# A four-layer graph network on one core: the last layer's weighted sums as seven products for eight, and its sums of weights as means

## The chip, the core and the metric

The kernel runs on one core of a Trainium2 chip. TensorE (PE) multiplies matrices out of SBUF into PSUM, VectorE (DVE) and ScalarE (ACT) work element by element on both memories, GpSimd (POOL) and SyncE (SP) here mostly issue DMAs. The metric is the device time of one execution, in microseconds (us); the time of a kernel is the median of several runs.

## What is computed

Four attention layers over a graph of 4096 nodes with 256 features each; after each one x becomes layernorm(x + layer(x)). The change concerns the fourth layer:

```python
def _L3_gnn_ref(features, adj, Wq, Wk):
    Qn = _cos_normalize(features @ Wq.T)          # 4096 x 128
    Kn = _cos_normalize(features @ Wk.T)
    raw_att = Kn @ Qn.T
    att = jnp.where(adj > 0, raw_att, NEG) * TEMP
    att = jax.nn.softmax(att, axis=1)
    prop_fea = att @ features                     # 4096x4096 @ 4096x256
    adj_mask = (jnp.sum(adj, axis=1) > 0).astype(features.dtype)[:, None]
    prop_fea = adj_mask * prop_fea + (1.0 - adj_mask) * features
    return (1.0 - KEEP_RATIO) * prop_fea + KEEP_RATIO * features   # KEEP_RATIO 0.5
x = _layernorm(x + _L3_gnn_ref(x, adj, Wq, Wk), axis=-1)
```

Every node is its own neighbour, so adj_mask is 1 and the last line before the layernorm is 1.5 x + 0.5 att @ x. The layernorm takes away each row's mean, so a constant added to all features of a row changes nothing in the output.

## The kernel before

All is in f32. The features stay in SBUF as X, 32 tiles of 128 nodes by 256 features, with a 257th column that holds 2.0. The nodes that are computed are taken in NB = 8 blocks of QW = 512 (QB = 4 tiles of 128); in each block a loop runs over all NT = 32 tiles of neighbours. A step of that loop, a unit (b, j), belongs to block b and tile j of neighbours.

In the fourth layer (`cosine_attention`, L887) a unit has two parts. `weights(b, j)` (L907) multiplies the turned keys and queries in T into a PSUM bank p of 128 neighbours by 512 nodes (L912), takes exp on ACT into a tile prob in SBUF (L916), and multiplies by the mask on DVE (L917). The mask is bf16; POOL loads it by DMA, four tiles at a time (`load_mask`, L849), into four buffers. `sums(b, j)` (L922) adds prob times features: for each of the block's four tiles k one matmul holds 128 by 128 of prob and streams X[:, j, :] of 257 columns (`one_sum`, L919). The 257th column gives twice the sum of the weights, which carries the factor 0.5. There are four accumulators acc0 to acc3 of one PSUM bank each. Two banks (pz) and two more (ps) serve the scores in turn; in block 0 only pz does.

The main loop (L982) calls weights for unit i and sums for unit i - LAG, with LAG = 2. After a block's last unit `outputs(b)` (L940) takes each accumulator: reciprocal of the sum (L931), multiply and add to 1.5 x (L932), mean and variance (L934, L935); then normalise (L176) and one store. 1.5 x was written to y by ACT (L994) eight units earlier. In the last block the sums of the last LAST = 4 units are held back and ordered by k, so that the first tiles are finished beside the last sums (`ending`, L947).

No order is written out for PE in this layer; a planner orders each engine's work, taking what is ready, and among that what comes first in the program. For `ending` DVE and ACT keep the program's order. Each engine works in order through what the planner gave it. The tiles of a pool are handed out in turn, and a tile is free for its next use when all reads of its last one are done.

The layer's start overlaps the end of the third (`additive_one`, L401): its outputs for the last block (`tail`), and `Cosine.prepare` for the last two blocks (L856). This turns X by DVE and DMA, multiplies by the weights w3_sb of the layer (L869), takes the rows' norms, and turns the result by DVE and DMA into T. w3_sb, 256 features by 128 query and 128 key columns, is loaded by `Cosine.start` (L836) in block 0 of the third layer. Each block of the third layer ends in `layernorm_block` (L182), which makes X's rows of mean 0 and variance 1.

Of the kernel before, what the change touches and what calls it, by code (L numbers as in the profile page):

```python
# [9 lines left out]
FP = mybir.dt.float32  # L10
# [3 lines left out]
AF = mybir.ActivationFunctionType  # L14
# [14 lines left out]
def kernel(  # L29
# [32 lines left out]
    def pool(stack, name, bufs, **kw):  # L62
        return stack.enter_context(tc.tile_pool(name=name, bufs=bufs, reuse_waits="tile", **kw))
# [118 lines left out]
    def layernorm_block(b, mv):  # L182
        normalise([X[:, b * QB + k, :D] for k in range(QB)], mv)

# [216 lines left out]
    def additive_one(w_sb, slope, tail, op, follow):  # L401
# [3 lines left out]
        with ExitStack() as lay:  # L405
# [68 lines left out]
            def outputs(b, k):  # L474
                if k == 0:
                    mvs[b] = fin.tile([P, QB, 2], FP, name="mv")
                add_elu(taken[b, k], b, k, mvs[b])
                if k == QB - 1:
                    layernorm_block(b, mvs[b])

            def even_bank():
                n = next(even) % QB
# [4 lines left out]
            with tc.manual_schedule(engines={mybir.EngineType.PE}):  # L487
                xTs = {0: turn(0), 1: turn(1)}
                project(0, xTs[0])
                project(1, xTs[1], [0, 1])  # L490
                fill_row(0)
                project(1, xTs[1], [2, 3])
                for i in range(len(units) + 1):
                    if i < len(units):
                        b, j = units[i]
                        weights(b, j)

                        if b == 0 and j // QB + 2 < NB:
# [329 lines left out]
    class Cosine:  # L828
# [7 lines left out]
        def start(self):  # L836
# [9 lines left out]
            load_w(self.w_sb[:, :, :P], wq3T, nc.sync)  # L846
            load_w(self.w_sb[:, :, P:], wk3T, nc.sync)

        def load_mask(self, b, m, seen=None):  # L849

            mask = self.mask[b, m] = self.masks.tile([P, self.MJ, QW], BF, name="mask")
            part = adjT.rearrange("(t p) i -> p t i", p=P)[:, m * self.MJ:(m + 1) * self.MJ, b * QW:(b + 1) * QW]
            with behind(seen) if seen is not None else nullcontext():
                nc.gpsimd.dma_start(mask, part)  # L854
# [30 lines left out]
                             nc.gpsimd if b < NB - 2 else nc.sync)  # L885

    def cosine_attention(co, tail):  # L887
        MJ = co.MJ

        LAST = 4  # L890
        T = [t.rearrange("p k (n i) -> p n k i", n=2) for t in co.T]
        with ExitStack() as lay:
            sb = pool(lay, "co_sb", LAST + 2)
            yp = pool(lay, "co_y", 2)
            co.turning = (pool(lay, "co_turn", 2), pool(lay, "co_squares", 1),
                          pool(lay, "co_turn_far", 2, space=bass.MemoryType.DRAM))

# [4 lines left out]
            acc, prob, y = {}, {}, {}  # L902

            def bank():
                return ps.tile([P, QW], FP, name="g")

            def weights(b, j):  # L907
                m = b, j // MJ
                if m not in co.mask:
                    co.load_mask(*m)  # L910
                p = bank() if b and j % 2 else pz.tile([P, QW], FP, name="p")
                nc.tensor.matmul(p.rearrange("p (k i) -> p k i", k=QB), T[j // QB][:, 0, j % QB], T[b][:, 1],  # L912
                                 start=True, stop=True)

                z = prob[b, j] = sb.tile([P, QW], FP, name="prob")
                nc.scalar.activation(z, p, AF.Exp)  # L916
                nc.vector.tensor_tensor(z, z, co.mask[m][:, j % MJ, :], OP.mult)  # L917

            def one_sum(b, j, k):  # L919
                nc.tensor.matmul(acc[b][k], prob[b, j][:, k * P:(k + 1) * P], X[:, j, :], start=(j == 0), stop=(j == NT - 1))  # L920

            def sums(b, j):  # L922
                if j == 0:
                    acc[b] = [pa.tile([P, D + 1], FP, name=f"acc{k}") for k in range(QB)]
                for k in range(QB):
                    one_sum(b, j, k)

            def sums_and_rest(b, k, mv):

                rden = fin.tile([P, 1], FP, name="rden1")  # L930
                nc.vector.reciprocal(rden, acc[b][k][:, D:])  # L931
                nc.vector.scalar_tensor_tensor(y[b][:, k, :], acc[b][k][:, :D], rden, y[b][:, k, :], OP.mult, OP.add)  # L932
# [14 lines left out]
            def ending(b):  # L947


                mv = {k: fin.tile([P, n, 2], FP, name=f"mv_end{k}") for k, n in ((0, 2), (2, 1), (3, 1))}  # L950
                roots = {}

# [10 lines left out]
                for k in range(QB):  # L963
                    for j in range(NT - LAST, NT):
                        one_sum(b, j, k)
                sums_and_rest(b, 0, mv[0][:, 0, :])
                sums_and_rest(b, 1, mv[0][:, 1, :])
                roots[0] = begin_root(mv[0])
                sums_and_rest(b, 2, mv[2][:, 0, :])
                finished(0, 2)  # L970
                roots[2] = begin_root(mv[2])
                sums_and_rest(b, 3, mv[3][:, 0, :])
                v, r, _ = begin_root(mv[3])
                finished(2, 1)
                end_root(v, r, 1)
                scale_row(y[b][:, 3, :], mv[3], r, 0)
                store(b, 3, 1, nc.scalar)

            units = [(b, j) for b in range(NB) for j in range(NT)]
            LAG = 2  # L980
            steps = {(0, j + n): (NB - 2 + b, step) for b, j in enumerate((1, 12)) for step, n in enumerate((0, 5, 8))}
            for i in range(len(units) + LAG):  # L982
                if i < len(units):
                    b, j = units[i]
                    weights(b, j)
                    if (b, j) == (0, 1):
                        tail(bank)
                    if (b, j) in steps:
                        co.prepare(bank, *steps[b, j])
                if i >= LAG:  # L990
                    b, j = units[i - LAG]
                    if j == NT - 8:
# [102 lines left out]
```

## Time and profile before

| | us |
|---|---|
| median of 3 runs | 2892.93 (2892.83 to 2893.68) |
| span of the profiled execution | 2890.8 |
| fourth layer, first score to the end of the span | from 2212.9 |
| score, one pass of 512 columns, 512 of them (L912) | 0.592 each |
| sum, one pass of 257 columns, 2048 of them (L920) | 0.380 each |
| exp of 512 (L916) | 0.597 each |
| mask multiplication of 512 (L917) | 0.690 each |
| last sum's start, last scaling's start, last store's issue | 2883.4, 2887.35, 2887.80 |

[...] one starts before the last has ended; so the work of PE is counted from starts to starts. A row of the profile names line, engine, operation, tiles written and read, shape and count; then the busy time in us and the mean of one in ns; after the second bar the idle time of that engine just before such instructions, and what ended it. PEld is the loading of the operand that PE holds. The granted clock is 0.999 of full speed over the span.

### The profile page before, as it was taken

What the parts mean: (1) busy time and instruction counts of PE and PEld (TensorE: products, weight loads), DVE (VectorE), ACT (ScalarE), POOL (GpSimd) and SP (SyncE); (2) the same over time, 40 slices, a digit from 0 to 9 for tenths busy, and PEclk for the clock granted to TensorE, in tenths of its full rate; (3) what the DMA queues carried; (4) which work ended last, traced back from release to release, by engine and by line L of the source; (5) the groups of instructions that cost most, each with busy time, mean ns of one, the idle gap of its engine ahead of it and who ended that gap; (6) DMA issues with size and microseconds to landing.
All of it is one profiled execution on the core that took longest, in us unless ns stands there. A gap on an engine that the chain in (4) does not pass through costs nothing.

```text
span 2890.8 us, 50566 instructions
## 1 busy us (share of the span) xinstructions
PE 2879.6 (100%) x20093; PEld 1548.7 (54%) x20093; DVE 1959.5 (68%) x2557; ACT 1652.8 (57%) x2582; POOL 945.9 (33%) x705
## 2 busy tenths in 40 slices
PE   9999999999999999999999999999999999999999
PEld 4333333333543333333333358888888777777776
DVE  8899999998777777777777765655667323333333
ACT  7899999997356666666666653444444222222222
POOL 0010010100068988989899870000002000000000
PEclk9999999999999999999999999999999999999999
DMA  7566667675269989889899885565566434333441
GB/s 206 103 139 137 142 134 145 138 133 92 88 138 192 183 187 196 181 187 190 182 193 188 181 178 133 164 184 158 159 185 178 76 57 58 59 58 59 59 59 30
DMA packets 237087, 398.04 MB, mean 138 GB/s; under 512 B 20929, under 2 KB 121265, under 8 KB 235954
## 3 DMA queue, kind: packets, MB, share of 16 engines
q0 software_dynamic: 104320, 184.06, 40.1%
q1 hardware_dynamic: 132112, 210.36, 23.7%
q8 instruction: 157, 2.57, 0.3%
q14 instruction: 80, 0.66, 0.1%
q10 hardware_dynamic: 418, 0.40, 0.0%
HBM read 328.60 MB, written 32.58 MB: 125 GB/s over the span
## 4 chain that ended last, share of the span: by engine, by line
PE 99%; DVE 1%; ACT 0%; DMA 0%; issue 0%; SPq 0%; DVEq 0%
PE acc L293 23%; PE acc L920 15%; PE acc L697 15%; PE p L664 15%; PE acc L464 8%; PE g L464 8%; PE p L912 4%; PE g L912 3%; PE g L579 2%; PE g L196 1%; PE pv L598 1%; PE acc L869 1%; PE acc L196 1%; PE g L118 1%; PE g L305 0%; PE p L734 0%
## 5 line engine op out<-in xcount | busy, mean ns | idle before, releaser
L676 DVE TENSOR_TENSOR prob<-p,mask 128x1024 f32<-128x1024 f32 x512 | 624.0, 1223 | 209.4 <-ACT p L666 203.6
L666 ACT ACTIVATE p<-p,shift 128x1024 f32<-128x1024 f32 x512 | 556.2, 1088 | 325.2 <-PE p L664 324.4
L293 PE MATMUL acc<-prob,V 128*32 128x512 f32 x6144 | 664.0, 593 | 1.1 <-DVE prob L283 1.1
L683 POOL TENSOR_TENSOR den<-den,prob 128x1024 f32<-128x1024 f32 x248 | 626.4, 2526 | 73.9 <-DVE prob L676 66.6
L280 ACT ACTIVATE prob<-row,dst 128x512 f32<-128x512 f32 x1020 | 633.1, 712 | 0.1
L283 DVE SCALAR_TENSOR_TENSOR prob<-prob,mask 128x2048 f32<-128x2048 f32 x256 | 582.7, 2287 | 24.2 <-ACT prob L280 21.3
L664 PE MATMUL p<-qT,kT 64*64 64x512 f32 x4096 | 532.7, 590 | 0.8 <-DVE prob L676 0.8
L697 PE MATMUL acc<-prob,V 64*64 64x512 f32 x4096 | 531.8, 590 | 0.0
L920 PE MATMUL acc<-X,prob 128*128 128x257 f32 x2048 | 485.4, 380 | 0.0
L920 PEld LDWEIGHTS acc<-X,prob 128*128 128x128 f32 x2048 | 389.2, 190 | 161.6 <-issue 112.3
L917 DVE TENSOR_TENSOR prob<-prob,mask 128x512 f32<-128x512 f32 x256 | 176.7, 690 | 405.6 <-ACT prob L916 405.4
L293 PEld LDWEIGHTS acc<-prob,V 128*32 128x32 f32 x6144 | 197.8, 110 | 452.6 <-issue 431.9
L91 POOL COPY tick<-prob 128x1 f32<-128x1 f32 x35 | 40.2, 1150 | 996.0 <-DVE prob L283 644.5
L456 ACT ACTIVATE e<-row,dst 128x512 f32<-128x512 f32 x256 | 184.1, 721 | 241.7 <-DVE prob L458 212.7
L697 PEld LDWEIGHTS acc<-prob,V 64*64 64x64 f32 x4096 | 156.0, 133 | 285.2 <-issue 277.9
L664 PEld LDWEIGHTS p<-qT,kT 64*64 64x64 f32 x4096 | 154.6, 133 | 277.2 <-issue 261.4
L458 DVE SCALAR_TENSOR_TENSOR prob<-e,mask 128x512 f32<-128x512 f32 x256 | 175.5, 686 | 169.8 <-PE acc L464 92.4
L854 POOL DMA_DIRECT2D mask<-in_adjT x64 | 48.1, 751 | 585.2 <-DVE prob L917 523.6
L689 POOL DMA_DIRECT2D den<-prob x240 | 233.2, 972 | 15.7 <-DVE prob L676 6.7
L916 ACT ACTIVATE prob<-p 128x512 f32<-128x512 f32 x144 | 85.7, 596 | 258.4 <-PE p L912 244.3
L464 PE MATMUL acc<-V,prob 128*128 128x257 f32 x1024 | 225.1, 380 | 0.0
L464 PE MATMUL g<-V,prob 128*128 128x257 f32 x1024 | 223.7, 380 | 0.0
(165 smaller groups left out, 1937.1 us busy)
## 6 DMA issues: line engine op xcount, KB each, us to landing
mask<-in_adjT SPq DMA_DIRECT2D x256, 512.0 KB
den<-prob POOLq DMA_DIRECT2D x240, 512.0 KB, 5.1
mask<-edges SPq DMA_DIRECT2D x512, 64.0 KB
mask<-in_adjT POOLq DMA_DIRECT2D x64, 512.0 KB, 5.7
edges<-in_adj POOLq DMA_DIRECT2D x32, 512.0 KB, 9.8
far<-squares SPq DMA_DIRECT2D x16, 512.0 KB
den<-prob SPq DMA_DIRECT2D x16, 512.0 KB
row<-far SPq DMA_DIRECT2D x7, 1024.0 KB
```

Of the source, the lines that this page charges most:

```text
L280: nc.scalar.activation(z[:, h, :], r, AF.Relu, bias=-1.0, scale=dst[:, j, h:h + 1])
L283: nc.vector.scalar_tensor_tensor(z, z, 1.0, mask[m][:, j % MJ, :].unsqueeze(1).to_broadcast([P, H, QW]), OP.add, OP.mult)
L293: nc.tensor.matmul(acc[b][h * G:(h + 1) * G, n, :], part, prob[b, j][:, h, :], start=(j == 0), stop=(j == NT - 1))
L464: nc.tensor.matmul(acc[b][k][:, :D + 1], prob[b, j][:, k * P:(k + 1) * P], V[:, j, :], start=(j == 0), stop=(j == NT - 1))
L664: nc.tensor.matmul(p[c * d:(c + 1) * d, r, :], kT[half, c, at:at + d], qT[half, c, cols], start=True, stop=True)
L666: nc.scalar.activation(p, p, AF.Exp, bias=shift)
L676: nc.vector.tensor_tensor(z, p, mask[m][:, j % MJ, :].unsqueeze(1).to_broadcast([P, KC, QW]), OP.mult)
L683: nc.gpsimd.tensor_tensor(to, to, flat, OP.add)
L689: nc.gpsimd.dma_start(to, flat, accum_op=OP.add)
L697: nc.tensor.matmul(acc[b][c][r * d:(r + 1) * d, :], V[half, j, r * d:(r + 1) * d], prob[b, j][half, r, :], start=(j == 0), stop=(j == NH - 1))
L912: nc.tensor.matmul(p.rearrange("p (k i) -> p k i", k=QB), T[j // QB][:, 0, j % QB], T[b][:, 1], start=True, stop=True)
L920: nc.tensor.matmul(acc[b][k], prob[b, j][:, k * P:(k + 1) * P], X[:, j, :], start=(j == 0), stop=(j == NT - 1))
```

## The change

The third layer leaves X with rows of mean 1 instead of 0 (`lift`: the subtracted mean is lowered by the variance plus epsilon, times the inverse root). From the weights w3_sb `centre` subtracts the mean over the features, so that queries and keys are what they were. Since features now have mean 1, the mean over a row of weights times features is the sum of the weights; the column of 2.0 isn't multiplied any more in this layer.

The sums are formed the other way round: features are held and weights streamed, so an accumulator has 128 features by 512 nodes, turned against before. For a pair g of neighbour tiles (even and odd), the two tiles, two halves of the features and two halves of the block's nodes make a product of 2 by 2 blocks; seven products of combinations of the halves replace the eight. `mix_features` forms four combinations of the features once, in block 0, and keeps them; `weights(b, g)` forms four of the weights for each pair on DVE. The accumulator is one tile of four banks, of which seven halves are used. `parts` adds these up into the four quarters of the result, `turned` turns them back by eight transposes into two ps banks, `halves_of_inverse` takes the mean of each row for the reciprocal. LAG is 4 units, LAST 3 pairs.

```diff
-    def normalise(ys, mv):
+    def normalise(ys, mv, lift=False):
         v, r, n = begin_root(mv)
         end_root(v, r, n)
+        if lift:
+
+            nc.vector.tensor_tensor(v, v, r, OP.mult)
+            nc.vector.tensor_tensor(mv[:, :, 0], mv[:, :, 0], v, OP.subtract)
...
+                        if (b, j) == (0, 12):
+                            follow.centre(bank())
...
+        def centre(self, pm):
+
+            w = self.w_sb
+            for c in range(KC):
+                nc.tensor.matmul(pm[:, :2 * P], ones, w[:, c, :], start=(c == 0), stop=(c == KC - 1))
+            for c in range(KC):
+                nc.vector.scalar_tensor_tensor(w[:, c, :], pm[:, :2 * P], -1.0 / D, w[:, c, :], OP.mult, OP.add)
...
+            sb = pool(lay, "co_sb", LAST + 1)
...
+            def mix_features(q):
+
+                x = X[:, 4 * q:4 * q + 4, :D].rearrange("p (g n) (h f) -> p g n h f", n=2, h=2)
+                t = mixed[q] = keep.tile([P, 2, 4, P], FP, name=f"mixed{q}")
+                nc.vector.tensor_tensor(t[:, :, 0, :], x[:, :, 0, 1, :], x[:, :, 0, 0, :], OP.subtract)
+                nc.vector.tensor_tensor(t[:, :, 1, :], x[:, :, 1, 1, :], t[:, :, 0, :], OP.add)
...
+            def scores(b, j):
...
                 p = bank() if b and j % 2 else pz.tile([P, QW], FP, name="p")
...
+                if j % 2 == 0:
+                    prob[b, j // 2] = sb.tile([P, 2, QW], FP, name="prob")
+                nc.scalar.activation(prob[b, j // 2][:, j % 2, :], p, AF.Exp)
+
+            def weights(b, g):
+
+                if b == 0 and g % 2 == 0:
+                    mix_features(g // 2)
+                z, lo = prob[b, g], 2 * g % MJ
+                nc.vector.tensor_tensor(z, z, co.mask[b, 2 * g // MJ][:, lo:lo + 2, :], OP.mult)
+                s = mix[b, g] = sb.tile([P, 4, HW], FP, name="mix")
+                nc.vector.tensor_tensor(s[:, :2, :], z[:, 0, :].rearrange("p (h i) -> p h i", h=2), z[:, :, HW:],
+                                        OP.subtract)
+                nc.vector.tensor_tensor(s[:, 2, :], z[:, 0, :HW], s[:, 1, :], OP.subtract)
+                nc.vector.tensor_tensor(s[:, 3, :], z[:, 1, :HW], s[:, 2, :], OP.subtract)
+
+            def product(b, g, n):
...
+                at, half, w, a = ((3, 0, even[:, :P], z[:, 0, :HW]), (0, 0, odd[:, :P], z[:, 1, :HW]),
+                                  (0, 1, t[:, 1], s[:, 2]), (1, 0, t[:, 0], s[:, 1]), (1, 1, odd[:, P:], s[:, 3]),
+                                  (2, 0, t[:, 2], s[:, 0]), (2, 1, t[:, 3], z[:, 1, HW:]))[n]
+                nc.tensor.matmul(acc[b][:, at, half * HW:(half + 1) * HW], w, a, start=(g == 0 and half == 0),
+                                 stop=(g == NP - 1), skip_group_check=True)
+
+            def first_parts(b):
+                a = acc[b]
+                one = cp.tile([P, HW], FP, name="one")
+                nc.scalar.copy(one, a[:, 3, :HW])
+                r = cp.tile([P, 2, HW], FP, name="r")
+                nc.vector.tensor_tensor(r, one.unsqueeze(1).to_broadcast([P, 2, HW]),
+                                        a[:, 0, :].rearrange("p (h i) -> p h i", h=2), OP.add)
+                return r, cp.tile([P, 2, HW], FP, name="u")
+
+            def parts(b):
+
+                a = acc[b]
+                r, u = first_parts(b)
+                nc.vector.tensor_tensor(u, r[:, 1:, :].to_broadcast([P, 2, HW]), a[:, 1:3, :HW], OP.add)
+                nc.vector.tensor_tensor(r[:, 1, :], u[:, 1, :], a[:, 1, :HW], OP.add)
+                nc.vector.tensor_tensor(u, u, a[:, 1:3, HW:], OP.add)
+                return r, u
+
+            def turned(r, u, h):
+
+                po = bank().rearrange("p (k f) -> p k f", f=D)
+                for k in range(2):
+                    for c, quarter in enumerate((r[:, 0], u[:, 0]) if h == 0 else (u[:, 1], r[:, 1])):
+                        nc.tensor.transpose(po[:, k, c * P:(c + 1) * P], quarter[:, k * P:(k + 1) * P], ident)
+                return po
...
             def outputs(b):
+                r, u = parts(b)
                 mv = fin.tile([P, QB, 2], FP, name="mv")
-                for k in range(QB):
-                    sums_and_rest(b, k, mv[:, k, :])
+                for h in range(2):
+                    po = turned(r, u, h)
+                    rden = halves_of_inverse(po)
+                    for k in (2 * h, 2 * h + 1):
+                        rest(b, k, po, rden, mv[:, k, :])
                 normalise([y[b][:, k, :] for k in range(QB)], mv)
                 store(b, 0, QB, nc.sync)
...
-                for k in range(QB):
-                    for j in range(NT - LAST, NT):
-                        one_sum(b, j, k)
...
+                for n in range(5):
+                    for g in range(NP - LAST, NP):
+                        product(b, g, n)
+                r, u = first_parts(b)
+                nc.vector.tensor_tensor(u[:, 0, :], r[:, 1, :], a[:, 1, :HW], OP.add)
+                nc.vector.tensor_tensor(u[:, 0, :], u[:, 0, :], a[:, 1, HW:], OP.add)
+                po = turned(r, u, 0)
+                for n in (5, 6):
+                    for g in range(NP - LAST, NP):
+                        product(b, g, n)
+                rden = halves_of_inverse(po)
+                for k in range(2):
+                    rest(b, k, po, rden, mv[0][:, k, :])
                 roots[0] = begin_root(mv[0])
...
-            LAG = 2
+            LAG = 4
...
-                    if i - LAG < len(units) - LAST:
-                        sums(b, j)
+                    if i - LAG < len(units) - 2 * LAST:
+                        for n in range(7)[:4] if j % 2 == 0 else range(7)[4:]:
+                            product(b, j // 2, n)
                         if j == NT - 1:
                             outputs(b)
```

`halves_of_inverse` is a reduction over the 256 features of two tiles at once, a multiplication and a reciprocal; `rest` is the multiply and add, the mean and the variance of one tile, as in `sums_and_rest` before. In `ending` the second half follows in the same way: three additions of 256 elements, four transposes, reduction, two times `rest`.

More of the change, by code (lines that the diff above doesn't have):

```diff
@@ L174, in scale_row, with layernorm_block @@
         nc.vector.tensor_scalar(y, y, mv[:, k, 0:1], r[:, k:k + 1], OP.subtract, OP.mult)
-    def normalise(ys, mv):
+    def normalise(ys, mv, lift=False):
         v, r, n = begin_root(mv)
         end_root(v, r, n)
+        if lift:
+            nc.vector.tensor_tensor(v, v, r, OP.mult)
+            nc.vector.tensor_tensor(mv[:, :, 0], mv[:, :, 0], v, OP.subtract)
         for k, y in enumerate(ys):
             scale_row(y, mv, r, k)
-    def layernorm_block(b, mv):
-        normalise([X[:, b * QB + k, :D] for k in range(QB)], mv)
+    def layernorm_block(b, mv, lift=False):
+        normalise([X[:, b * QB + k, :D] for k in range(QB)], mv, lift)
     def additive_values(xT, b, groups, w_sb, V, src, dst, H, slope):
@@ L478, in outputs @@
                 if k == QB - 1:
-                    layernorm_block(b, mvs[b])
+                    layernorm_block(b, mvs[b], lift=True)
             def even_bank():
@@ L888, in cosine_attention @@
         MJ = co.MJ
-        LAST = 4
+        NP = NT // 2
+        HW = QW // 2
+        LAST = 3
         T = [t.rearrange("p k (n i) -> p n k i", n=2) for t in co.T]
         with ExitStack() as lay:
-            sb = pool(lay, "co_sb", LAST + 2)
+            keep = pool(lay, "co_mixed", 1)
+            sb = pool(lay, "co_sb", LAST + 1)
             yp = pool(lay, "co_y", 2)
+            cp = pool(lay, "co_parts", 1)
             co.turning = (pool(lay, "co_turn", 2), pool(lay, "co_squares", 1),
@@ L901, in cosine_attention @@
             ov = out.rearrange("(t p) d -> p t d", p=P)
-            acc, prob, y = {}, {}, {}
+            mixed, acc, prob, mix, y = {}, {}, {}, {}, {}
             def bank():
                 return ps.tile([P, QW], FP, name="g")
[L907 to L910, printed above, removed]
+            def mix_features(q):
[3 more added lines that the diff above has]
+                nc.vector.tensor_tensor(t[:, :, 1, :], x[:, :, 1, 1, :], t[:, :, 0, :], OP.add)
+                nc.vector.scalar_tensor_tensor(t[:, :, 2, :], x[:, :, 1, 1, :], -1.0, x[:, :, 0, 1, :],
+                                               OP.mult, OP.subtract)
+                nc.vector.tensor_tensor(t[:, :, 3, :], x[:, :, 1, 0, :], t[:, :, 1, :], OP.subtract)
+            def scores(b, j):
+                if (b, j // MJ) not in co.mask:
+                    co.load_mask(b, j // MJ)
                 p = bank() if b and j % 2 else pz.tile([P, QW], FP, name="p")
@@ L913, in weights @@
                                  start=True, stop=True)
[L915 to L924, printed above, removed]
-                for k in range(QB):
-                    one_sum(b, j, k)
@@ L928, in sums_and_rest @@
[L928 to L932, printed above, removed]
+                if j % 2 == 0:
[11 more added lines that the diff above has]
+                nc.vector.tensor_tensor(s[:, 3, :], z[:, 1, :HW], s[:, 2, :], OP.subtract)
@@ new lines, in product @@
+            def product(b, g, n):
+                z, s, t = prob[b, g], mix[b, g], mixed[g // 2][:, g % 2]
+                even, odd = X[:, 2 * g, :D], X[:, 2 * g + 1, :D]
+                at, half, w, a = ((3, 0, even[:, :P], z[:, 0, :HW]), (0, 0, odd[:, :P], z[:, 1, :HW]),
[3 more added lines that the diff above has]
+                                 stop=(g == NP - 1), skip_group_check=True)
@@ new lines, in turned, with halves_of_inverse @@
+            def turned(r, u, h):
[4 more added lines that the diff above has]
+                return po
+            def halves_of_inverse(po):
+                rden = fin.tile([P, 2], FP, name="rden2")
+                nc.vector.tensor_reduce(rden, po, AX.X, OP.add)
+                nc.vector.tensor_scalar_mul(rden, rden, 2.0 / D)
+                nc.vector.reciprocal(rden, rden)
+                return rden
@@ L933, in sums_and_rest, with rest @@
+            def rest(b, k, po, rden, mv):
+                nc.vector.scalar_tensor_tensor(y[b][:, k, :], po[:, k % 2, :], rden[:, k % 2:k % 2 + 1], y[b][:, k, :],
+                                               OP.mult, OP.add)
                 st = fin.tile([P, 6], FP, name="bn")
@@ L947, in ending @@
             def ending(b):
+                a = acc[b]
                 mv = {k: fin.tile([P, n, 2], FP, name=f"mv_end{k}") for k, n in ((0, 2), (2, 1), (3, 1))}
@@ L961, in finished @@
                     store(b, k, n, nc.sync)
-                for k in range(QB):
-                    for j in range(NT - LAST, NT):
-                        one_sum(b, j, k)
-                sums_and_rest(b, 0, mv[0][:, 0, :])
-                sums_and_rest(b, 1, mv[0][:, 1, :])
+                for n in range(5):
[11 more added lines that the diff above has]
+                    rest(b, k, po, rden, mv[0][:, k, :])
                 roots[0] = begin_root(mv[0])
-                sums_and_rest(b, 2, mv[2][:, 0, :])
+                nc.vector.tensor_tensor(u[:, 1, :], r[:, 1, :], a[:, 2, :HW], OP.add)
+                nc.vector.tensor_tensor(r[:, 1, :], u[:, 1, :], a[:, 1, :HW], OP.add)
+                nc.vector.tensor_tensor(u[:, 1, :], u[:, 1, :], a[:, 2, HW:], OP.add)
+                po = turned(r, u, 1)
                 finished(0, 2)
+                rden = halves_of_inverse(po)
+                rest(b, 2, po, rden, mv[2][:, 0, :])
                 roots[2] = begin_root(mv[2])
-                sums_and_rest(b, 3, mv[3][:, 0, :])
-                v, r, _ = begin_root(mv[3])
+                rest(b, 3, po, rden, mv[3][:, 0, :])
+                v, w, _ = begin_root(mv[3])
                 finished(2, 1)
-                end_root(v, r, 1)
-                scale_row(y[b][:, 3, :], mv[3], r, 0)
+                end_root(v, w, 1)
+                scale_row(y[b][:, 3, :], mv[3], w, 0)
                 store(b, 3, 1, nc.scalar)
             units = [(b, j) for b in range(NB) for j in range(NT)]
-            LAG = 2
+            LAG = 4
             steps = {(0, j + n): (NB - 2 + b, step) for b, j in enumerate((1, 12)) for step, n in enumerate((0, 5, 8))}
@@ L984, in cosine_attention @@
                     b, j = units[i]
-                    weights(b, j)
+                    scores(b, j)
+                    if j % 2:
+                        weights(b, j // 2)
                     if (b, j) == (0, 1):
@@ L991, in cosine_attention @@
                     b, j = units[i - LAG]
+                    if j == 0:
+                        acc[b] = pa.tile([P, 4, QW], FP, name="acc")
                     if j == NT - 8:
```

## The prediction

> **What bounds the kernel now.** I read the page's busy shares and its chain first, then the fourth layer by windows, then the chain in order of time, then the timeline of one block's end. From the page, the busy shares, the chain by engine, and the two costly groups of this layer:
>
> ```profile
> PE 2879.6 (100%) x20093; PEld 1548.7 (54%) x20093; DVE 1959.5 (68%) x2557; ACT 1652.8 (57%) x2582; POOL 945.9 (33%) x705
> ...
> PE 99%; DVE 1%; ACT 0%; DMA 0%; issue 0%; SPq 0%; DVEq 0%
> ...
> L920 PE MATMUL acc<-X,prob 128*128 128x257 f32 x2048 | 485.4, 380 | 0.0
> ...
> L917 DVE TENSOR_TENSOR prob<-prob,mask 128x512 f32<-128x512 f32 x256 | 176.7, 690 | 405.6 <-ACT prob L916 405.4
> ```
>
> TensorE (PE) is 99% of the chain. The sums (L920) count 2048 instructions for 1024 calls: an f32 matmul runs as two passes, so I price a pass. VectorE (DVE) waits 405 us in front of its mask multiplications, always for earlier work. The windows of blocks 0 and 2 (columns: length, busy time of PE, PEld, DVE, ACT, POOL, granted clock, DMA share, GB/s):
>
> ```profile
> 2212.00:2225.00 13.00, 13.00 (x49) 8.85 (x48) 12.56 (x38) 6.77 (x14) 0.76 (x1) 1.00 0.29 73
> 2225.00:2240.00 15.00, 15.00 (x61) 11.31 (x61) 10.30 (x25) 4.97 (x22) 0.76 (x1) 1.00 0.70 148
> ...
> 2386.00:2469.00 83.00, 83.00 (x322) 60.91 (x321) 27.69 (x57) 20.46 (x35) 5.93 (x8) 1.00 0.40 58
> ```
>
> In a middle block DVE works 27.7 of 83 us. At the layer's start it works 22.9 of 28 us. There is room later and almost none at the start. The chain in order of time gives a block's length, and the starts of PE groups that a price can be taken from:
>
> ```profile
> 2390.41 2.60 PE acc L920 x12
> 2473.35 2.60 PE acc L920 x12
> 2556.28 2.60 PE acc L920 x12
> ```
>
> Blocks start 82.93 us apart. Over 32 tiles of features that is 2.592 us per tile, the same as inside a block, so the ends of blocks cost PE nothing now. Twelve passes take 2.60 us, 0.2167 each; a tile is 8 of those (1.733) and two score passes (0.859 together). Why nothing is lost shows in the timeline of a block's end:
>
> ```profile
> 2469.70 0.69 DVE L917 TENSOR_TENSOR prob<-prob,mask 128x512 f32<-128x512 f32 x1
> 2470.31 0.48 DVE L932 SCALAR_TENSOR_TENSOR y<-acc,rden,y 128x256 f32<-128x256 f32 x1
> ...
> 2470.60 1.02 PE L912 MATMUL p<-T,T 128*128 128x512 f32 x2
> ...
> 2471.46 1.03 PE L920 MATMUL acc<-X,prob 128*128 128x257 f32 x4
> ...
> 2472.33 1.02 PE L912 MATMUL g<-T,T 128*128 128x512 f32 x2
> ...
> 2473.18 2.77 PE L920 MATMUL acc<-X,prob 128*128 128x257 f32 x12
> ```
>
> The four accumulators are separate tiles, each free after one reciprocal and one L932. PE takes two of the next block's sums, then a score, then the rest. The planner moves ready work forward past work that must wait.
>
> [...]L880 1224, L917 690, L213 420. [...]
>
> **The change, part by part.** Prices for new PE work come from rows of the same shape:
>
> ```profile
> L869 PE MATMUL g<-w_sb,xT x32: 378/379/380, 2229.6 to 2261.3; 128*128 128x256 f32 x32
> ```
>
> [...]In the timeline 16 of these passes start at 2229.58 and L920 follows at 2233.03: 0.2156 each, with one weight load (190 ns) for each hidden beside the pass before. A new product has just this shape: 128 by 128 held, 256 columns streamed. Eight transposes (L118) start at 1754.13 and sums follow at 1755.00: 0.109 each.
>
> 1. Products. A pair of tiles costs 2 x 2.592 = 5.184 us now. Afterwards: two scores 1.718, and 7 products of two passes, 14 x 0.2156 = 3.018; 4.736. Saved 0.448, times 128 pairs: **-57.3 us**, all on the path. The column of weight sums (257th) goes with it.
> 2. Turning the outputs: 8 transposes x 8 blocks x 0.109 = **+7.0** on PE.
> 3. Centring the weights in layer 3: four passes, **+0.9** on PE. Its two DVE operations are beside PE work; the weight loads were issued at 1733, well before. The lift adds two small DVE operations (0.16 each) to each of eight blocks, beside PE's sums: nothing; without cover 2.6.
> 4. Weights on DVE: a pair costs 1.224 + 0.690 + 2 x 0.42 = 2.75 instead of 1.38, in 4.74 us of PE. With LAG 4, from the end of a pair's second score to its first product PE has 2 scores and 10 products, and the next score: about 6.9 us. Exp (0.6 after 0.2) and all of DVE's work need 3.6. Steady state: nothing. Sums per block: 16 x 2.75 = 44, plus outputs of about 11, 55 of 78 us; DVE doesn't become the bound. The mask loads move into scores() on POOL's queue; a load lands 5.7 us after its issue, and four buffers of four tiles hold some 28 us of work ahead: nothing.
> 5. Block 0. DVE's other work in 2212:2303 is 43.3 us busy less 32 x 0.69 = 21.2, of which some 16 before 2240. Added: mixing features, 32 operations of 256 elements, 13.5 us, and 22 for the weights. From 2215 DVE must do the first pair (4.1 with its mix), then the third layer's last outputs and preparation (16 in all), then pairs 1 to 3 (2.5 each back to back, and one mix). I get the fourth pair's weights at about 2242. PE's work up to its products is scores for 14 tiles (12.0), three pairs of products (9.1) and one preparation (3.6): 24.7 us from 2213, with prob's four buffers letting no more scores ahead. 2242 less 2238 is 4, and the gaps of ACT's part in the outputs add; **+7**, bounds 2 and 11. Later in the block DVE needs 6.6 of every 9.5 us and nothing more is lost.
> 6. Seven block ends. The accumulator is now one tile of four banks, free for the next block's first product only after all of parts(): the ACT copy (L722's copy of that size: 375 ns) and 0.69 can run early, but after the last product remain 0.69 + 0.42 + 0.69 = 1.8. Ahead of these on DVE stand the next block's second pair, whose exp ends about 0.5 before the last product: 2.75 less 0.5 = 2.3. So parts end about 4.2 after the last product. PE has meanwhile two scores on the pz banks (1.72); the other scores need ps banks that the turned outputs claim. Idle 2.5 at this order; 0.8 if the planner gives ps to scores first; up to 4.5 if the scores don't move. Afterwards two pairs of products (6.0) with three scores cover the 7.7 us of DVE outputs, just. I take 2.0 x 7 = **+14**, bounds 6 and 32. Before, this was 0.
> 7. The end. Now the last product's passes end near 2883.8 and the last scaling starts at 2887.35. Afterwards the first half's reduction and rest (3.5 us, begun about 1.5 before the last product ends) stand ahead of three steps of 0.42, four transposes, a reduction (L588: 678 ns), two rests of 1.1, and the roots: last scaling done about 9.9 after the last product instead of 4; the store's 3 us are the same. **+6**, bounds 4 and 8.
>
> Sum: -57.3 + 7.0 + 0.9 + 7 + 14 + 6 = -22.4. The profiled execution's span is 2890.8, so 2868.4; the median of the runs stands 2.1 above that span, so **2870.5 us**.
>
> **Rivals.** (A) The forecast. (B) The planner hides both block 0 and the block ends: scores move ahead, DVE puts parts() first. For it: before hides exactly such a burst (7.5 us of DVE). Against: one release for four banks. Only items 1, 2, 3, 7 and some 3 us remain: -57.3 + 7.9 + 6 + 3 = -40.4, 2852.5. (C) Both at their upper ends: -57.3 + 7.9 + 11 + 32 + 8 = +1.6, about 2894: no change. (D) Slower: at each block end the release, the outputs and the next weights run as one DVE queue: 2.3 for the pair ahead, 1.8 for parts, 7.7 and normalise's 2.7 before the third pair can be weighted, with ps banks held so scores stop: 14.5 against 6 of products, 8.5 x 7 = 60 in place of 14: 2914 span, 2916. It decides from about 6 us lost per end. For it: two ps banks serve both scores and turned outputs. Against: even tiles' scores use pz alone, and DVE has 40% free.
>
> **How the numbers follow.** A 0.61, B 0.20, C 0.11, D 0.08. Less than 0.2% (5.8 us) from before can't be told from no change with this kernel. A and B are faster: with a sliver of C, 0.82; C is mostly no change, 0.10; D 0.08. The range from B's time to the inner edge of C, 2851 to 2889, leaves out D, most of C and a tail below B.
>
> **What would show it.** Right: products with 256 columns at 0.216 a pass and a pair at 4.74 us inside blocks; PE gaps of some 2 us at seven block ends, waiting for the last u of parts(); gaps of some 7 us in the first 30 us of the layer; a tail some 6 us longer. Wrong: DVE gaps vanish in middle blocks (4), a pair above 4.8 us in mid-block (1), or block ends above 6 us (D).

## The result and the profile after

The changed kernel takes 2856.45 us (2856.10 to 2857.02, 4 runs) beside 2892.88 for the kernel before on the same chip (2892.63 to 2893.68): a ratio of 0.9874, with a 95% interval of 0.986 to 0.9888. That is 36.4 us less. The forecast was 22.4 less (2870.5, range 2851 to 2889), and the rival B stood at 2852.5. The time lies in the range, and is much nearer to B. The span of the profiled execution went from 2890.8 to 2854.5.

The page of the changed kernel: busy shares, the chain by engine, and two groups. The new products have four groups in all, by what they hold and stream; one is shown.

```profile
PE 2832.5 (99%) x19905; PEld 1503.5 (53%) x19905; DVE 2168.0 (76%) x2913; ACT 1653.4 (58%) x2590; POOL 945.3 (33%) x705
...
PE 97%; DVE 2%; ACT 0%; issue 0%; DMA 0%; ACTq 0%
...
L952 DVE TENSOR_TENSOR prob<-prob,mask 128x1024 f32<-128x1024 f32 x128 | 156.4, 1222 | 165.9 <-ACT prob L945 165.8
...
L966 PE MATMUL acc<-mix,mixed 128*128 128x256 f32 x768 | 206.9, 379 | 0.0
```

VectorE does 208.5 us more than before and TensorE 47 less, and PE still is the chain. VectorE's 2% of the chain (1% before) are for the most part the seven block ends, with some 4.6 us each, and the tail, with some 12.7. The windows of part of block 0 and of a middle block (columns as before: length, then busy PE, PEld, DVE, ACT, POOL, clock, DMA share, GB/s):

```profile
2225.00:2240.00 15.00, 15.00 (x60) 11.10 (x59) 15.00 (x42) 5.52 (x23) 0.76 (x1) 1.00 0.34 50
2240.00:2255.00 15.00, 15.00 (x58) 10.70 (x57) 15.00 (x31) 3.96 (x7) 1.48 (x2) 1.00 0.80 164
...
2305.00:2382.40 77.40, 76.89 (x298) 55.33 (x297) 52.31 (x96) 20.53 (x36) 5.92 (x8) 1.00 0.43 62
```

In block 0 VectorE is busy all the time for 30 us, and yet PE doesn't stop. A middle block is 77.4 us with 0.5 us of idle PE in it. The chain in order of time has the same three block starts as the one of before:

```profile
2304.86 2.59 PE acc L966 x12
...
2382.28 2.59 PE acc L966 x12
...
2459.69 2.59 PE acc L966 x12
```

77.41 us a block, where it was 82.93. Pairs inside a block start 4.738 us apart (4.74 in the chain, 2249.85 to 2254.59; forecast 4.736). Sixteen pairs make 75.81, eight transposes 0.87, together 76.68; so a block end costs 0.73 us beyond PE's own work. That this is so little has its reason in the timeline of PE at the end of block 0, from the last products to the next block's first:

```profile
2299.24 0.59 PE L966 MATMUL acc<-prob,mixed 128*128 128x256 f32 x2
2299.67 1.88 PE L941 MATMUL p<-T 128*128 128x512 f32 x4
2301.38 0.27 PE L992 MATMUL g<-ident,r 128*128 128x128 f32 x1
2301.49 1.88 PE L941 MATMUL p<-T,T 128*128 128x512 f32 x4
2303.88 0.33 PE L992 MATMUL g<-ident,u 128*128 128x128 f32 x1 [0.50 <-DVE u L984]
...
2304.70 1.03 PE L966 MATMUL acc<-prob,X 128*128 128x256 f32 x4
```

Eight passes of p stand in the gap, which are four scores of the next block, all on the pz banks. The last u of parts() (L984) ends 4.15 us after 2299.67, where PE starts what follows the last product. Four scores and one transpose cover 3.55 of it (eight passes at 0.43 and 0.109), and PE waits 0.50. Counted from starts, as all work of PE is here, the gap is 0.66: by these spacings the four scores and the transpose last to 2303.22, and the next instruction starts at 2303.88.

The tail is in the timeline of all engines, first PE's wait and the products held to the last, then the last scaling:

```profile
2831.17 1.99 PE L966 MATMUL acc<-prob,X 128*128 128x256 f32 x8 [1.08 <-DVE prob L952]
...
2838.24 0.33 PE L992 MATMUL g<-ident,r 128*128 128x128 f32 x1 [1.19 <-DVE r L974]
...
2839.14 0.33 PE L992 MATMUL g<-ident,u 128*128 128x128 f32 x1 [0.58 <-DVE u L1045]
...
2840.83 1.46 PE L966 MATMUL acc<-prob,mixed 128*128 128x256 f32 x6
...
2851.02 0.41 DVE L174 TENSOR_SCALAR y<-y,mv_end,r 128x256 f32<-128x256 f32 x1
```

The last pass begins at about 2841.9 (five spacings of 0.216 after 2840.83). From there to the last scaling are 9.1 us, where it was 3.95; and PE waited ahead of it in three places, 2.9 us as the lines show it and 3.4 counted from starts.

### The profile page after: what moved, and what is told of

Read it like the earlier page. It is cut to its first block, busy times and chain, and to the rows that moved or that the text cites. A ratio compares the mean times of both kernels' runs of the same rounds, so it can differ in the third digit from the quotient of the medians.

```text
span 2854.5 us, 50462 instructions
## 1 busy us (share of the span) xinstructions
PE 2832.5 (99%) x19905; PEld 1503.5 (53%) x19905; DVE 2168.0 (76%) x2913; ACT 1653.4 (58%) x2590; POOL 945.3 (33%) x705
## 4 chain that ended last, share of the span: by engine, by line
PE 97%; DVE 2%; ACT 0%; issue 0%; DMA 0%; ACTq 0%
PE acc L297 23%; PE p L670 15%; PE acc L703 15%; PE acc L966 13%; PE acc L468 8%; PE g L468 8%; PE p L941 3%; PE g L941 3%; PE g L585 2%; PE g L200 1%; PE pv L604 1%; PE acc L883 1%; PE acc L200 1%; PE g L118 1%; PE g L309 0%; DVE prob L952 0%
## 5 line engine op out<-in xcount | busy, mean ns | idle before, releaser
L952 DVE TENSOR_TENSOR prob<-prob,mask 128x1024 f32<-128x1024 f32 x128 | 156.4, 1222 | 165.9 <-ACT prob L945 165.8
L468 PEld LDWEIGHTS g<-V,prob 128*128 128x128 f32 x1024 | 194.3, 190 | 27.7
L468 PEld LDWEIGHTS acc<-V,prob 128*128 128x128 f32 x1024 | 193.6, 190 | 27.6 <-issue 0.4
L966 PE MATMUL acc<-mix,mixed 128*128 128x256 f32 x768 | 206.9, 379 | 0.0
## 6 DMA issues: line engine op xcount, KB each, us to landing
edges<-in_adj POOLq DMA_DIRECT2D x32, 512.0 KB, 10.1
```

Of the source, the lines that this page charges most:

```text
L468: nc.tensor.matmul(acc[b][k][:, :D + 1], prob[b, j][:, k * P:(k + 1) * P], V[:, j, :], start=(j == 0), stop=(j == NT - 1))
L966: nc.tensor.matmul(acc[b][:, at, half * HW:(half + 1) * HW], w, a, start=(g == 0 and half == 0), stop=(g == NP - 1), skip_group_check=True)
```

## A measure for small differences

In the profiled executions the fourth layer's first score starts between 2212.7 and 2215.8, in kernels whose first three layers do the same work. Where less than 2 us matter I use the fourth layer alone: from its first score's start to the issue of the last store. This comes from one profiled execution of each kernel, so how well it repeats isn't known; dve_program, whose median is that of the change, differs by 0.46.

| kernel | median, us | fourth layer, us | block period, us |
|---|---|---|---|
| before | 2892.88 | 674.86 | 82.93 |
| changed | 2856.45 | 638.23 | 77.41 |
| plain_eight | 2904.00 | 685.37 | 83.28 |
| bufs3 | 2862.59 | 644.63 | 78.28 |
| dve_program | 2856.59 | 637.77 | 77.41 |
| mix_twice | 2858.19 | 639.57 | 77.41 |
| dve_program2 | 2874.85 | 657.04 | 77.42 |
| mix_weights_twice | 2860.37 | 641.26 | 77.68 |
| split_acc | 2849.27 | 630.28 | 76.69 |
| split_and_order | 2848.27 | 630.40 | 76.69 |
| hold_four | 2848.24 | 629.43 | 76.69 |

The block period is the distance of the starts of the next two blocks' first products. The kernel before ran beside the experiments at 2892.2 to 2892.6.

## Experiment 1: eight plain products in the new layout

Features are held, weights streamed, outputs turned and sums taken as means, as in the change; but the products are the plain ones, with no mixing. The accumulator then needs two banks and has two buffers, `parts` is four copies, and the ending holds its sums without splitting them in two. The product, out of the whole edit:

```diff
...
+            def product(b, g, n):
+                j, f = 2 * g + n // 2, n % 2
+                nc.tensor.matmul(acc[b][:, f, :], X[:, j, f * P:(f + 1) * P], prob[b, g][:, n // 2, :],
+                                 start=(j == 0), stop=(j == NT - 1))
...
```

> The changed kernel with features held, weights streamed, outputs turned and means in place of sums, but with the eight plain products (four matmuls of 512 columns for a pair of tiles) and without the mixing on VectorE; accumulators in two buffers of two banks. Theory (the whole gain is the eighth product that is left out): 1024 columns in two passes more for a pair less 896, 128 pairs x 2 x 0.2156 = 55 us more than the changed kernel, less some 5 us that its block ends cost: 2904 us, so some 10 us slower than the kernel before, since turning (7), centring (1) and the longer tail (some 7) stay and the saved 257th column gives about 4. Rival (holding the features, or dropping the column of sums, brings a good part by itself): below 2890 us.

Measured 2904.0 us (ratio to before 1.0038, interval 1.0023 to 1.0053). The theory's number came out. A block is 83.28 us there, and sixteen pairs of 5.15 with eight transposes of 0.109 make 83.3, so its block ends cost nothing. Against this kernel, leaving out the eighth product is worth 47.6 us, net of the mixing and of what the block ends then cost, and carries the whole gain; the new layout by itself, with its longer ending, costs 11 us. It has to be paid to use the seven products in this form.

## Experiment 2: one score fewer at a block's end

```diff
-            sb = pool(lay, "co_sb", LAST + 1)
+            sb = pool(lay, "co_sb", LAST)
```

> Changed kernel with three buffers instead of four for weights and mixed weights; nothing else. In the order of instructions one score fewer (three instead of four) stands between a block's last product and the transposes. Theory (the release of the accumulator comes 4.1 us after the last product as forecast, and PE covers it with scores moved ahead, two of them written out by exp and two parked in the pz banks): each of seven block ends loses one score more, 0.86 us, so +6 us, about 2862.5 us, idle PE 1.4 us at a block end instead of 0.5. Rival (the release itself is early and scores don't matter): within 1 us of 2856.5.

The same pool holds the weights and the mixed weights, three buffers each now. Measured 2862.6 us, 6.1 more, with 78.28 us a block: 0.87 more, the price of one score (0.86). PE at the same place as above:

```profile
2301.10 1.88 PE L941 MATMUL p<-T 128*128 128x512 f32 x4
2302.82 0.27 PE L992 MATMUL g<-ident,r 128*128 128x128 f32 x1
2302.93 1.02 PE L941 MATMUL p<-T,T 128*128 128x512 f32 x2
2305.32 0.33 PE L992 MATMUL g<-ident,u 128*128 128x128 f32 x1 [1.36 <-DVE u L984]
```

Three scores instead of four, and PE waits 1.36 instead of 0.50 for the same L984. The release of the accumulator is as late as forecast; what stands in the gap was counted too low. The two pz banks served four scores in the gap of the changed kernel: the exp of the first starts at 2300.72 and takes 0.60, the third score starts after it, at 2301.49, and the second exp at 2301.58. With four buffers for prob these two scores are written out and two wait in the banks; the next exp starts at 2308.35.

## Experiment 3: VectorE held to the program's order in block 0

Two runs. In the first each step of the loop had its own block of fixed order:

```diff
             for i in range(len(units) + LAG):
+              with tc.manual_schedule(engines={mybir.EngineType.DVE}) if i < 16 else nullcontext():
```

> Changed kernel, with VectorE held to the program's order in the first 16 units of block 0, so that the third layer's last outputs stand ahead of the weights of pairs 1 and later. Theory (my forecast of 7 us lost in block 0 failed because the order isn't the program's: the planner puts what PE needs first and defers the outputs): +4 to +9 us, 2861 to 2865 us, with PE idle in the first 30 us of the layer. Rival (there was more room on VectorE than I counted): within 1 us of 2856.5.

Measured 2856.6 us, no change. By itself this spoke for the rival, but the trace showed that the run didn't test the theory: the order was held only within a step. The timeline of VectorE there has the mask multiplication of pair 1 before the third layer's first output is taken further (L214):

```profile
2218.88 1.22 DVE L952 TENSOR_TENSOR prob<-prob,mask 128x1024 f32<-128x1024 f32 x1
...
2221.29 0.29 DVE L214 TENSOR_SCALAR neg<-o 128x256 f32<-128x256 f32 x1
```

In the second run one block of fixed order holds all 16 steps:

```diff
-            for i in range(len(units) + LAG):
+            def step(i):
...
+            with tc.manual_schedule(engines={mybir.EngineType.DVE}):
+                for i in range(16):
+                    step(i)
+            for i in range(16, len(units) + LAG):
+                step(i)
```

> Changed kernel with VectorE held to the program's order in one piece over the first 16 steps of block 0 (the run before held it step by step, and its trace still had pair 1's weights ahead of the third layer's outputs). Theory (the 7 us that I charged to block 0 are those of the program's order; the planner avoids them by deferring the outputs and the preparation of the last tiles): +4 to +9 us, 2861 to 2865 us, PE idle before the weights of pairs 1 to 3. Rival (PE can do without them longer than I counted): within 1 us of 2856.5.

Measured 2874.9 us, 18.4 more. The timeline of PE:

```profile
2221.30 5.91 PE L941 MATMUL p<-T,T 128*128 128x512 f32 x12
2235.08 2.07 PE L966 MATMUL acc<-prob,X 128*128 128x256 f32 x4 [7.87 <-DVE prob L952]
...
2249.75 1.02 PE L941 MATMUL p<-T,T 128*128 128x512 f32 x2
2255.70 2.08 PE L966 MATMUL acc<-prob,X 128*128 128x256 f32 x4 [4.92 <-DVE prob L952]
```

PE runs out of work twice, 7.9 and 4.9 us, and both times waits for a mask multiplication: the first stands behind the third layer's outputs, the second behind the preparation of the last tiles, whose norms themselves wait for PE's L883 (VectorE stands 7.64 us in front of them, up to 2249.40). The direction is the theory's, the size twice its upper end. I had not counted the second wait, nor that PE was slow after both pauses, at 0.465 a pass instead of 0.216 at first, which adds some 4.8 us for the two (last section). The size isn't that of the program's order alone either: between 2215.28 and 2222.89 VectorE does three mixings of features (twelve operations) that stand behind pair 1's weights in the program's order; that they come from the steps after the sixteenth, which were not held, is likely but not shown. So an order near the program's on VectorE does cost what I feared and more; the changed kernel doesn't have that order.

## Experiment 4: more work on VectorE

Features mixed twice, in block 0 only; then the first mixing of the weights twice, in all blocks. The second edit:

```diff
+                for _ in range(2):
+                    nc.vector.tensor_tensor(s[:, :2, :], z[:, 0, :].rearrange("p (h i) -> p h i", h=2), z[:, :, HW:],
+                                            OP.subtract)
```

> Changed kernel with every mixing of features in block 0 computed twice: 32 operations of 256 elements more on VectorE, 13.3 us of work, all in block 0. Theory (VectorE is full from 2212 to 2257 and PE gets its weights just in time there): +3 to +8 us, 2859.5 to 2864.5 us. Rival (the work is covered, there is room): +0 to +1 us.

Measured 2858.2 us, 1.7 more, and 1.3 more in the fourth layer, 0.9 of it in block 0: between the two theories, nearer to the rival. Of 13 us of work in a stretch where VectorE has no gap, a tenth came through. It isn't the full stretch that counts: work that PE doesn't need soon moves on into the rest of the block, where there was room. In the 15 us from 2255 and the 15 from 2270 VectorE works 11.4 and 10.1 us in the changed kernel, and 15.0 in both here.

> Changed kernel with the first mixing of the weights (512 elements, 0.69 us) computed twice for each pair: 128 x 0.69 = 88 us more on VectorE, which then works some 63 of 77 us in a middle block. Theory (inside a block the work on VectorE is covered; at a block's end the weights of the next block's second pair stand ahead of parts(), so the release comes 0.69 later and each of seven ends loses 0.7): +4 to +7 us, 2860.5 to 2863.5, PE idle at a block end 1.2 instead of 0.5 us, pairs inside a block still 4.74. Rival (VectorE is near its limit): +15 us or more, with pairs longer than 4.74. Third (the weights ahead don't matter): within 1.5 us of 2856.5.

Measured 2860.4 us, 3.9 more (3.0 in the fourth layer). VectorE works 62.5 of 77.7 us in a middle block. The total is just below the theory's lower end, but its mechanism isn't what was measured: a block end lost 0.27 (PE waits 0.77 for the last u instead of 0.50), not 0.7. In the changed kernel the steps of parts() and of the mixing alternate (2300.34 to 2303.14) and don't simply queue. My estimate is that the doubled step takes the place of a shorter one, which moves behind the last u; this run's order on VectorE isn't shown. Seven ends give 1.9, the rest came in block 0. Pairs stay at 4.74, so VectorE isn't near its limit.

## Experiment 5: the accumulator in three tiles

```diff
-                        acc[b] = pa.tile([P, 4, QW], FP, name="acc")
+                        acc[b] = (pa.tile([P, QW], FP, name="acc0"), pa.tile([P, 2, QW], FP, name="acc12"),
+                                  pa.tile([P, QW], FP, name="acc3"))
...
```

> Changed kernel with the accumulator as three tiles (bank 3; bank 0; banks 1 and 2) in place of one tile of four banks. Theory (the wait is by tile, not by bank: the ACT copy of bank 3 starts only after the last product into any bank, and the next block's first product waits for the last addition of parts()): the copy and r move ahead of the last products, the next block's first three products fill the gap, PE's idle 0.5 us at seven ends goes, and the tail is shortened by about 1.2: -4 to -6 us, 2850.5 to 2852.5 us. Rival (the planner's order or the chain on VectorE sets it, not the tile): within 1 us of 2856.5.

Measured 2849.3 us (ratio to before 0.9852, interval 0.9837 to 0.9866), 7.2 less than the change. The block period is 76.69, PE's own work to 0.01 us; seven ends of 0.72 give 5.0 and the tail gave the rest, 2.9 in the fourth layer alone, where 1.2 was expected. The timeline of the end of block 0, with the copy (L973) and r (L975) ahead of the last products, and the next block's products in the gap:

```profile
2298.15 0.37 ACT L973 COPY one<-acc 128x256 f32<-128x256 f32 x1
...
2299.02 0.69 DVE L975 TENSOR_TENSOR r<-one,acc 128x512 f32<-128x512 f32 x1
...
2300.90 0.59 PE L967 MATMUL acc<-prob,mixed 128*128 128x256 f32 x2
2301.33 0.27 PE L993 MATMUL g<-ident,r 128*128 128x128 f32 x1
2301.44 1.02 PE L941 MATMUL p<-T 128*128 128x512 f32 x2
...
2302.30 1.03 PE L967 MATMUL acc<-prob,X 128*128 128x256 f32 x4
```

Here the copy starts 0.27 us after the last product into its bank (two passes from 2297.45 to 2297.88), and the next block's first products start at 2302.30, 1.58 before the last addition of parts() (L985, 2303.88). In the changed kernel the same copy starts at 2299.87, 0.2 after the last products (2299.67), though the bank that it reads got its last product some 3.4 us before these (2295.79 to 2296.22):

```profile
2299.87 0.37 ACT L972 COPY one<-acc 128x256 f32<-128x256 f32 x1 [0.70 <-PE acc L966]
2300.34 0.68 DVE L974 TENSOR_TENSOR r<-one,acc 128x512 f32<-128x512 f32 x1
```

So in this program the wait was for the tile, in both directions, and splitting the tile removed it.

## Experiment 6: the tail

On top of the three tiles, the held products of the last pair after those of the two pairs before it; then also four pairs held, with five buffers.

```diff
-                for n in range(5):
-                    for g in range(NP - LAST, NP):
-                        product(b, g, n)
+                for gs in (range(NP - LAST, NP - 1), range(NP - 1, NP)):
+                    for n in range(5):
+                        for g in gs:
+                            product(b, g, n)
...
```

> As split_acc, and in the ending the held products of the last pair come after those of the two pairs before it, instead of product by product over all three. Theory (in the changed kernel PE stands 1.1 us there for the last pair's weights): 1 us less than split_acc, 2849.5 to 2851.5. Rival (the tail is set by VectorE's chain alone, which starts with the last held product of banks 1): no less than split_acc.

Measured 2848.3 us, 1.0 less; but the fourth layer alone is 630.40 beside 630.28. The gain isn't in the part that was changed, so the rival stands: with three tiles the planner had already filled that gap, and the tail is VectorE's chain. The experiment so tests less than it was meant to.

> As split_and_order, with four pairs instead of three held back for the ending and five buffers instead of four. Theory (the tail is VectorE's chain of some 11.5 us, which starts when the held products of banks 0, 1 and 3 are done; what is held beyond that is PE work beside it): the last two products of four pairs instead of three come after that point, 3.4 us instead of 2.6 of PE work, so the end comes 0.9 us earlier: 2847.4 us. Rival (the tail waits for the last product): the same as split_and_order, 2848.3, within 0.4.

Measured 2848.2 us, the same; the fourth layer alone is 629.43, 0.97 less, which is the theory's 0.9, and PE's pause before the last four transposes goes from 2.37 to 1.51. With one execution of each this speaks for the theory and doesn't settle it: by the medians it is the rival's result. I count split_acc and its variants as one version, 2848 to 2849 us: 43 to 44 us below the kernel before.

## Why the forecast was right, and where its sizes were off

The time came out within the range, but the forecast's two largest losses didn't. Of 21 us for block 0 and the block ends 5.4 were measured, and both terms lie below their own lower bounds (2 and 6). What the traces show is in the main rival B, which had 0.20 against the forecast's 0.61: the planner hides block 0 and moves scores into the block ends. Only B's other half, parts() first on VectorE, isn't there; parts() alternates with the next weights. B's sum is 4 us too low, half of it at the block ends and half in the tail. Of the signs named, passes at 0.216, pairs at 4.74 and a wait for the last u of parts() came; gaps of 2 us at block ends were 0.66, and the gaps in the first 30 us of the layer weren't there. What was right is the gain, steps 1 to 3; the range was wide enough to hold B as well.

The fourth layer went from 674.86 to 638.23, by 36.6. Step 3 is in the third layer; against the steps of the forecast:

| step | forecast | measured | from |
|---|---|---|---|
| 1 products | -57.3 | -57.1 | pairs at 4.738 against 5.184 |
| 2 turning | +7.0 | +7.0 | 8 transposes a block, 0.87 |
| 3 centring | +0.9 | +0.87 | four passes in layer 3, no wait after them |
| 5 block 0 | +7 | +0.3 | as below, and the rest of the sum |
| 6 seven block ends | +14 | +5.1 | 0.73 each |
| 7 the end | +6 | +8.1 | 5.2 after the last pass, 3.4 of waits before, less 0.4 for four transposes that step 2 has |

- Steps 1 and 2, and the price of 0.2156 from the L869 row, held to 0.2 us. Experiment 1 shows that the gain lies in the product left out.
- Step 3 held; the four passes of the centring start at 1757.91 and L200 follows at 1758.78.
- Step 4 held: 52.3 us of VectorE in a block of 77.4 (forecast 55 of 78), and a fifth more of it cost 0.27 us per block end. The price of L880, 1224 ns for 1024 elements, came out as 1222 for L952, whose mask is bf16. The forecast's remark under rival D that VectorE has 40% free doesn't fit its own step 4, which leaves 30%; measured are 32%.
- Step 5 failed. PE's work from the first score to the last product of block 0 is 72 passes of scores, 8 of them for the next block, 224 of products and 32 of preparation, together 86.1 us; the trace has 86.4. I put "the third layer's last outputs and preparation (16 in all)" ahead of the weights of pairs 1 to 3. The timeline has them between and after (the lines stand below this list). Experiment 3 shows that an order near the program's would have cost 18 us; experiment 4 that even 13 us more work would nearly have fitted. That a resource is full for 30 us said nothing as long as part of what fills it could wait.
- Step 6 named the right wait and the right time (parts end "about 4.2 after the last product", measured 4.15) and mis-sized the cover: two scores where there were four, all on the pz banks. Experiment 2 takes one away and gets its price back. One detail of it was wrong without effect on the sum: the copy and r didn't run early, since the wait was by tile and not by bank (experiment 5: the copy began 3.6 us after the last product into its bank, with three tiles 0.27 after). That put r's 0.68 us behind the last product as well; that the mixing alternates with parts() made up for it, since eight steps of 5.2 us together took 4.6 (2299.20 to 2303.82).
- Step 7 was 2.1 too low: the span after the last pass came out shorter than forecast (5.2 more, not 6), and 3.4 us of PE's waits before it weren't in the sum. With the accumulator in three tiles these waits fall to 1.0, and the end comes 2.9 us earlier.

For step 5, the timeline of VectorE in the changed kernel, pair 2's mask multiplication and then the scaling of the last tiles of X:

```profile
2226.87 1.19 DVE L952 TENSOR_TENSOR prob<-prob,mask 128x1024 f32<-128x1024 f32 x1
...
2232.85 1.43 DVE L174 TENSOR_SCALAR X<-X,mv,r 128x256 f32<-128x256 f32 x4
```

The kernel before scaled these tiles seven microseconds earlier:

```profile
2225.76 1.38 DVE L174 TENSOR_SCALAR X<-X,mv,r 128x256 f32<-128x256 f32 x4
```

Block 0 and the block ends came out 6.7 and 8.9 better than forecast, and the tail 2.1 worse: 13.5 of the 14 us between forecast and result. The remaining half microsecond lies within the differences in the fourth layer's start.

## What to carry to other kernels

Seven products for eight paid here, where TensorE was 99% of the chain and VectorE had room; price them by passes, and add the turning back, the waits before the last products and the tail. When a full engine is to be charged with new work, ask what of its present work has to come first; only that is a delay. When a result is read in parts, try one tile per part: here the wait was for the whole tile, and three tiles in its place saved 7.2 us.

## What the runs showed that was not expected

TensorE was slow after two pauses. In the run with 7.9 and 4.9 us of idle PE (dve_program2), the four passes after the first pause take 1.86 us from start to start of what follows (2235.08 to 2236.94), 0.465 each instead of 0.216, and the spacing is normal again after about 5 us. The windows of that run (columns as before) show the granted clock with it, the third number from the end:

```profile
2225.00:2240.00 15.00, 7.00 (x16) 4.31 (x17) 12.96 (x36) 1.73 (x5) 0.76 (x1) 0.66 0.32 65
```

It was 1.00 in the window before and 0.95 in the one after. The twelve passes from 2235.08 to 2240.08 take 5.0 us, where they would take 2.6 at 0.216; so the pause cost some 2.4 us more than itself, and the second pause likewise (twelve passes from 2255.70 to 2260.64, in a window with a clock of 0.82). A clock of 2.6/5.0 while these passes ran, and of 1.00 before them, would leave 0.84 in the window above; by this estimate the clock was low in the pause already. After pauses of 0.50 us (the changed kernel) and 1.36 (bufs3) at a block's end the next four passes are at 0.216 (2304.70 to 2305.56, 2306.14 to 2307.00).

The length of the pause alone didn't decide it. In the tail of the changed kernel PE pauses 2.36 us before the last four transposes, and these start 0.21 to 0.24 apart (2844.65 to 2845.31), at a clock of 0.50 between 2844.5 and 2845.5; in split_acc the same four follow a pause of the same 2.36 us 0.10 to 0.14 apart (2838.85 to 2839.20). In the 13 us before its pause the changed kernel had three more waits, 2.9 us together, and split_acc one of 0.86; whether this made the difference isn't shown.

On VectorE two instructions on the same operand stood further apart here than unrelated ones. In the tail the second of three additions of 256 elements reads the first one's result and the third reads and overwrites it; they start 0.45 us apart (2843.18, 2843.63, 2844.08) at 0.41 to 0.42 each. At a block's end, where parts() and mixing alternate, instructions of 0.42 start 0.33 to 0.34 apart (2302.14 to 2303.14) and those of 0.68 to 0.69 0.60 apart (2300.34, 2300.94, 2301.54). The additions of the tail read PSUM; the last two mixing steps of a pair, one on the other's result and both in SBUF, start 0.46 apart too inside block 0 (2296.45 and 2296.91). By my estimate from these spacings the planner's alternation made VectorE about 0.1 us per instruction faster than two chains in a row.
